# A gated cellular automaton beside the coupled map of its own image, its result in DRAM for the gate, and the gate's VectorE operations behind the first half of a map step

## The chip, the cores and the metric

The kernel runs on one core of a Trainium2 chip. The metric is device time in microseconds of one execution, lower is better. The page and the trace come from one profiled execution.

## The reference

Four layers run over 32 images of 8 channels, 256 x 256, each as `x = x + conv_i(group_norm(x))`. The change lies in layer 0; layers 1 to 3 (a quantized 3x3 convolution, a 3x3 convolution, a 5x5 box filter) stay as they are. Layer 0, cut to what matters:

```python
def _L0_conv_ref(x, K_local, Wp, bp, Wu, bu, Wg1, bg1, Wg2, bg2):
    drive = x[:, :C_OUT]
    grid = drive
    for _ in range(STEPS):                      # 15 steps
        mapped = R * grid * (1.0 - grid)
        local = _conv(mapped, K_local, groups=C_OUT)
        physics = (1.0 - EPS) * mapped + EPS * local
        grid = (1.0 - BETA) * physics + BETA * drive
    cml_out = jnp.clip(grid, 0.0001, 1.0 - 0.0001)
    h = jax.nn.relu(_conv(x, Wp, bp))           # 128 hidden channels
    nca_out = jax.nn.sigmoid(_conv(h, Wu, bu))
    gin = jnp.concatenate([x, cml_out, nca_out], axis=1)
    g = jax.nn.sigmoid(_conv(jax.nn.relu(_conv(gin, Wg1, bg1)), Wg2, bg2))
    return g * cml_out + (1.0 - g) * nca_out
```

So an image has three parts: the *map* (15 dependent steps giving `cml_out`), the *automaton* (`nca_out`, which depends on the normalized image alone), and the *gate*, which needs both.

## The kernel before, in words

**The map** is `lattice(b, ahead)`. The image is normalized (L346 into `flat`, L360 in place), turned by 32 TensorE transposes (L355), and six of the eight channels are stepped on TensorE, in two halves of three channels. For a half, TensorE multiplies the state by `patch_sb` (L391), then the ring of neighbours from other patches by `ring_sb` (L393); VectorE adds the drive (`psc`, L402); ScalarE squares into `state` (L419); `spread(half)` then issues four DMAs on SP's queue (L259), which fill `rings` for the same half of the next step. The other two channels are stepped by VectorE with nine taps (L338, over `strip` and `acc`): three taps in a step's first half, six in its second, where two closing operations (L412, L413) follow. After step 15 the result is turned back (L428, L431) and stored to `cr_d` (`store`, four DMAs on POOL's queue, and eight of SP's for the two VectorE channels).

**The automaton** is in `gated()`, in chunks `n` of 1/8 image; a chunk has four *batches*. `load` brings a batch's `im` tile in six DMAs on POOL's queue out of `xn_d`, where the normalized image lies in DRAM. Each batch has four matmuls `ph` (L633, 8 profile records), a relu to `hh` (L638), and a group of matmuls `pn` (L610). `close` turns the chunk's `pn` by a sigmoid into `nh` (L588), an SBUF tile with room for four chunks; the gate's neighbour rows are copied from it by `beside_blocks` (L480).

**The gate** is the generator `gate`: it loads its quarter of an image (`xq`, `cq`, the neighbours `above` and `below`, `xc`), issues 18 matmul records of `pg` (L531, L543), four with the neighbours (L539), a relu (L545), `pq` (L548), a sigmoid `gt` (L550), and seven VectorE operations (L561 to L568) that mix, add to `xc` and take statistics; the result goes to `x1_d` (L569). After an image's eighth gate its statistics are finished.

**What sets the order.** All of layer 0 is under a hand-written schedule: an instruction stands on its engine's queue where the Python code issues it. `lattice` yields gaps in microseconds of TensorE work to be filled; for each, the main loop draws pieces of `gated()`:

```python
for gap in lattice(b, ahead):
    if b > 0:
        left += gap
        while left > 0 and place[0] < b * NCH:
            left -= next(rest)
```

So during the map of image b the automaton and the gates of image b - 1 are issued, wherever they fall; the map of image 0 has nothing beside it, and the automaton and gates of image 31 come after the last map. `errands(b)` is drawn once a half: it writes image b to `xn_d` (four DMAs, L273) and `nr_d`, loads image b + 1 and takes its statistics. In its ScalarE part `lattice` issues, channel by channel, a square into `state` (L374) and the lift of the drive (L375), and then the `spread` of a half.

Of the kernel before, what the change touches and what calls it, by code (L numbers as in the profile page):

```python
# [18 lines left out]
C = 8  # L19
# [47 lines left out]
def kernel(  # L67
# [100 lines left out]
    with ExitStack() as es:  # L168
        wt = es.enter_context(tc.tile_pool(name="wt0", bufs=1))
        imp = es.enter_context(tc.tile_pool(name="im", bufs=4))  # L170
# [49 lines left out]
        nh = wt.tile([P, 8, WP], F32, name="nh")  # L220
# [7 lines left out]
        for t in (*xbs, nh, zero, strip):  # L228
            nc.gpsimd.memset(t, 0.0)
# [7 lines left out]
        nr_d = [dram.tile([P, HB, WP], F32, name=f"nr_d{i}") for i in range(3)]  # L237

        cr_d = [dram.tile([P, HB, WP], F32, name=f"cr_d{i}") for i in range(3)]
        for t in xn_d:  # L240
            nc.sync.dma_start(
                window(t, 0, [[HP * WP, C], [(HP - 1) * WP, 2], [1, WP]]),
                nh[0:C, 0:2, :],
            )
# [21 lines left out]
        def errands(b):  # L266
# [3 lines left out]
            if b >= 0:  # L270
                xb = xbs[b % 2]
                for r in four:
                    nc.gpsimd.dma_start(  # L273
                        window(
                            xn_d[b % 3], (1 + r.start) * WP,
                            [[HP * WP, C], [RB * WP, HB], [1, 4 * WP]],
                        ),
                        xb[:, r, :].rearrange("p r w -> p (r w)"),
                    )
                    yield  # L280
# [47 lines left out]
        def lattice(b, ahead):  # L328
# [8 lines left out]
            def tap(dy, dx):  # L337
# [8 lines left out]
            nc.vector.tensor_scalar(  # L346
                flat.rearrange("p (x r w) -> p r x w", x=TX, r=RB),
                xi.rearrange("p r (x w) -> p r x w", w=PW),
                st[:, 0:1], st[:, 1:2], ALU.subtract, ALU.mult,
            )  # L350
            yield 5
            for t4 in range(TX // 4):
# [6 lines left out]
                if t4 == 0:  # L359
                    nc.vector.tensor_scalar(  # L360
                        xi, xi, st[:, 0:1], st[:, 1:2], ALU.subtract, ALU.mult
                    )
                if t4 == 4 and b > 0:
                    store(b - 1)
                if t4 == 1:
# [4 lines left out]
                    edges()  # L370
                yield 1
            dr = flat.rearrange("p (x c y) -> p c x y", x=TX, c=C)
            for c in range(CP):
                nc.scalar.activation(inner(c), dr[:, c], AF.Square, bias=minus)  # L374
                nc.scalar.activation(  # L375
                    dr[:, c], dr[:, c], AF.Identity, bias=lift[:, c : c + 1], scale=BETA_
                )
                if c == 0:
                    nc.scalar.mul(d2, d2, BETA_)
                if c % HALF == HALF - 1:  # L380
                    spread(c // HALF)
                yield 1.5
            yield 4
            for step in range(STEPS):
                for half in range(2):
# [31 lines left out]
                    if step < STEPS - 1:  # L417
# [3 lines left out]
                        if half == 1:  # L421
                            edges()
                    next(ahead, None)
                    yield BLOCK - 1.7
            for t4 in range(TX // 4):
# [10 lines left out]
                )  # L436
                yield 1
# [25 lines left out]
        def beside_blocks(tiles, src, q, k0, n, slots):  # L463

            row = src.shape[1] * WP
            for i, (p, k) in enumerate(((P - C, k0 - 1), (0, k0 + 1))):
                to = tiles[i][q : q + 24, k0 % 4 : k0 % 4 + n, :].rearrange("p k w -> p (k w)")
                runs = []  # L470
                for j in range(n):
                    at = slots[k + j] if 0 <= k + j < HB else None
                    if runs and at is not None and runs[-1][2] is not None and at == runs[-1][2] + runs[-1][1]:
                        runs[-1][1] += 1
                    else:
                        runs.append([j, 1, at])
                for j, m, at in runs:
                    long = m * WP - 2
                    source, row_, start = (zero, WP, 0) if at is None else (src, row, p * row + at * WP)
                    nc.gpsimd.dma_start(  # L480
                        to[:, j * WP : j * WP + long],
                        window(source, start, [[row_, C], [1, 3], [1, long]]),
                    )

        place = [0]

        def gated():
# [5 lines left out]
            SLOTS = [k % 8 for k in range(HB)]  # L493
# [17 lines left out]
            def gate(n, quarter):  # L511
                b, r2 = divmod(n, NCH)
                k0 = 2 * r2
                if r2 % 2 == 0:
                    for name, t in (("xq", nr_d), ("cq", cr_d)):
# [3 lines left out]
                    for q, t in ((0, nr_d), (24, cr_d)):  # L519
                        beside_blocks(halos[n // 2], t[b % 3], q, k0, 4, range(HB))  # L520
                xc = hp.tile([P, 2, W], F32, name="xc", bufs=2)
                nc.gpsimd.dma_start(xc, xr_d[b % 3][:, k0 : k0 + 2, :])
                yield 0
                yield 0
                mine = slice(2 * (r2 % 2), 2 * (r2 % 2) + 2)
                xq, cq = (quarter[i][:, mine, :] for i in ("xq", "cq"))
                pg = ps_n.tile([P, 512], F32, name="pg", tag="pn")
                o = pg.rearrange("p (k w) -> p k w", w=W)
                for s, src in enumerate((xq, cq, nh[:, k0 % 8 : k0 % 8 + 2, :])):
# [14 lines left out]
                g1 = hp.tile([P, 512], F32, name="g1", tag="gt", bufs=2)  # L544
# [4 lines left out]
                gt = hp.tile([P, 2, W], F32, name="gt", tag="gt", bufs=2)  # L549
# [8 lines left out]
                ci = cq[:, :, 1 : 1 + W]  # L558
                ni = nh[:, k0 % 8 : k0 % 8 + 2, 1 : 1 + W]

                nc.vector.tensor_tensor(ci, ci, ni, ALU.subtract)  # L561
                nc.vector.tensor_tensor(gt, gt, ci, ALU.mult)
# [96 lines left out]
        with tc.manual_schedule():  # L659
# [15 lines left out]
            for _ in rest:  # L675
                pass
# [366 lines left out]
```

## Time and profile before

| what | value |
|---|---|
| median of 3 runs (lowest, highest) | 16326.91 us (16326.64, 16338.44) |
| profiled execution, its own time | 16318.33 us |
| its span, mean granted clock | 16316.6 us, 0.961 |
| PE, DVE, ACT, POOL busy | 95%, 72%, 35%, 34% |
| DMA | 2276.12 MB, 139 GB/s mean |
| first start of L346 for image 0, image 1 | 33.8, 381.7 us |
| last transposes back (L428); last gate sigmoid (L550) start | 13342.7; 13589.0 us |

The time of interest runs from the start to about 13,595 us, where layer 0 ends; the remaining 2,720 us are layers 1 to 3. The page cuts the span into 40 slices of some 408 us, close to one image of layer 0. PEclk in it is the granted share of TensorE's clock.

### The profile page before, as it was taken

The numbers are of one execution on the slowest core, as the hardware profiler recorded it, in microseconds if no ns is written. First come the engines' busy times: TensorE is split into PE (matmuls) and PEld (weight loads), VectorE is DVE, ScalarE is ACT, GpSimd is POOL, SyncE is SP. The second block draws the span as 40 slices with busy tenths as digits, with TensorE's granted clock in tenths as the row PEclk, the third lists the DMA queues.
The fourth block names the chain that finished last, engine by engine and source line by source line (L and its number), as shares of the span: only waits on it lengthen the run. The fifth ranks groups of instructions, "written<-read, shape, count | busy, mean of one in ns | idle before, by whom it ended". The sixth has DMA issues, their size and how long they took to land.

```text
span 16316.6 us, 141125 instructions
## 1 busy us (share of the span) xinstructions
PE 15452.2 (95%) x42888; PEld 6215.7 (38%) x42888; DVE 11705.9 (72%) x14652; ACT 5726.7 (35%) x8862; POOL 5598.2 (34%) x9491
## 2 busy tenths in 40 slices
PE   6999999999999999999999999999999997999999
PEld 2333333333333333333333333333333332333333
DVE  7777777777777777777777777777777764555554
ACT  2433444443434434443434444343444442111110
POOL 1333333333333333333333333333333342111111
PEclk7999999999999999999999999999999998999999
DMA  4766666666666666666666666666666664555554
GB/s 104 148 146 144 150 147 144 147 150 146 149 144 148 150 147 147 144 147 145 147 142 149 148 144 147 141 148 146 147 149 147 146 134 98 119 119 119 119 118 105
DMA packets 1057742, 2276.12 MB, mean 139 GB/s; under 512 B 419740, under 2 KB 623508, under 8 KB 1050724
## 3 DMA queue, kind: packets, MB, share of 16 engines
q0 software_dynamic: 704512, 1492.80, 40.6%
q1 hardware_dynamic: 352484, 774.29, 23.4%
q8 instruction: 356, 5.83, 0.2%
q14 instruction: 390, 3.19, 0.1%
HBM read 1078.04 MB, written 471.38 MB: 95 GB/s over the span
## 4 chain that ended last, share of the span: by engine, by line
PE 74%; DVE 13%; DMA 7%; ACT 3%; issue 2%; SPq 1%; POOL 0%; DVEq 0%; ACTq 0%; POOLq 0%
PE ph L633 17%; PE psc L391 14%; PE psc L393 13%; PE pg L531 9%; DVE acc L338 7%; PE psv L725 5%; PE pn L610 5%; PE psv L811 4%; DMA qb<-qh 3%; DMA rings<-state 2%; PE psv L729 2%; PE pq L548 1%; PE pg L543 1%; PE pg L539 1%; DVE psc L402 1%
## 5 line engine op out<-in xcount | busy, mean ns | idle before, releaser
L338 DVE SCALAR_TENSOR_TENSOR acc<-strip,taps_sb,acc 128x1024 f32<-128x1024 f32 x3840 | 4930.4, 1284 | 124.8 <-DMA strip<-strip 4.7
L505 POOL DMA_DIRECT2D im<-xn_d x6144 | 3458.3, 566 | 3250.0 <-PE ph L633 1434.7
L633 PE MATMUL ph<-im,wp_sb 72*128 72x512 f32 x8192 | 4091.7, 615 | 308.8 <-ACT hh L638 251.3
L638 ACT ACTIVATE hh<-ph,bp_sb 128x512 f32<-128x512 f32 x4096 | 2755.8, 690 | 4441.9 <-PE ph L633 4385.7
L402 DVE SCALAR_TENSOR_TENSOR psc<-psc,flat 128x512 f32<-128x512 f32 x2880 | 1921.4, 696 | 2813.0 <-PE psc L393 2797.2
L391 PE MATMUL psc<-state,patch_sb 128*128 128x512 f32 x5760 | 2812.0, 626 | 74.1 <-ACT state L419 63.3
L393 PE MATMUL psc<-rings,ring_sb 80*128 80x512 f32 x5760 | 2713.5, 607 | 129.8 <-DMA rings<-state 129.8
L633 PEld LDWEIGHTS ph<-im,wp_sb 72*128 72x128 f32 x8192 | 1489.5, 193 | 2425.4 <-issue 1587.8
L419 ACT ACTIVATE state<-psc,minus 128x512 f32<-128x512 f32 x2688 | 1690.2, 690 | 1818.8 <-DVE psc L402 1713.1
L391 PEld LDWEIGHTS psc<-state,patch_sb 128*128 128x128 f32 x5760 | 1114.5, 199 | 1696.2 <-issue 1375.7
L393 PEld LDWEIGHTS psc<-rings,ring_sb 80*128 80x128 f32 x5760 | 1114.7, 194 | 1576.8 <-issue 1545.7
L569 POOL DMA_DIRECT2D x_d<-xc x256 | 146.9, 574 | 3493.1 <-DVE xc L564 3416.6
L811 PE MATMUL psv<-xr,w_sb 128*128 128x512 f32 x2560 | 1162.9, 600 | 1.3 <-DVE xr L792 1.3
L610 PE MATMUL pn<-hh,wu_sb 128*32 128x512 f32 x8192 | 1133.9, 609 | 3.3 <-ACT hh L638 3.3
L776 POOL DMA_DIRECT2D x_d<-x x512 | 321.0, 643 | 1941.0 <-DVE x L770 1696.3
L725 PE MATMUL psv<-xh,w_sb 128*128 128x512 f32 x1536 | 753.0, 629 | 9.6 <-issue 9.6
L531 PE MATMUL pg<-xq,wg_sb 128*128 128x512 f32 x1536 | 749.3, 626 | 0.0
L754 ACT ACTIVATE x<-psv,b_sb,sc 128x512 f32<-128x512 f32 x256 | 199.3, 779 | 1466.2 <-PE psv L729 1465.8
L531 PE MATMUL pg<-cq,wg_sb 128*128 128x512 f32 x1536 | 713.7, 601 | 0.0
L811 PEld LDWEIGHTS psv<-xr,w_sb 128*128 128x128 f32 x2560 | 466.1, 189 | 610.8 <-issue 606.0
L338 DVE SCALAR_TENSOR_TENSOR acc<-strip,taps_sb,d 128x1024 f32<-128x1024 f32 x480 | 613.2, 1277 | 0.0
L831 DVE TENSOR_TENSOR y<-psv,y 128x512 f32<-128x512 f32 x256 | 177.1, 692 | 593.7 <-PE psv L811 593.7
(163 smaller groups left out, 12188.9 us busy)
## 6 DMA issues: line engine op xcount, KB each, us to landing
im<-xn_d POOLq DMA_DIRECT2D x6144, 96.6 KB, 6.6
rings<-state SPq DMA_DIRECT2D x1920, 159.5 KB
rings<-state SPq DMA_DIRECT2D x1920, 106.3 KB
strip<-strip SPq DMA_DIRECT2D x960, 126.0 KB
xn_d<-xb POOLq DMA_DIRECT2D x128, 516.0 KB, 7.7
nr_d<-xb POOLq DMA_DIRECT2D x128, 516.0 KB, 7.2
xq<-nr_d POOLq DMA_DIRECT2D x128, 516.0 KB, 5.1
cq<-cr_d POOLq DMA_DIRECT2D x128, 516.0 KB, 7.9
```

The lines of the kernel that those rows point to most:

```text
L338: nc.vector.scalar_tensor_tensor(acc, strip[:, dy : dy + RQ, dx : dx + W], taps_sb[:, 3 * dy + dx : 3 * dy + dx + 1], d2 if dy == 1 and dx ...
L391: nc.tensor.matmul(pss[-1], patch_sb[:, c, :], inner(c), start=True, stop=False)
L393: nc.tensor.matmul(pss[c % HALF], ring_sb[:, c, :], rings[half][:, c % HALF, 0 : TX * SY].rearrange("p (x y) -> p x y", y=SY)[:, :, 0:TY], ...
L402: nc.vector.scalar_tensor_tensor(ps, ps, FLOOR, dr[:, c], ALU.max, ALU.add)
L419: nc.scalar.activation(inner(c), pss[c % HALF], AF.Square, bias=minus)
L505: nc.gpsimd.dma_start(im[24 * dy : 24 * dy + 24, k, 0:run], window(xn_d[b % 3], at, [[HP * WP, C], [1, 3], [1, run]]),)
L531: nc.tensor.matmul(o, wg1_sb[:, s, dx, :], src[:, :, dx : dx + W], start=s == dx == 0, stop=False,)
L610: nc.tensor.matmul(pn[32 * q : 32 * q + 32, :], wu_sb[:, i, :], hh, start=i == 0, stop=i == 3,)
L633: nc.tensor.matmul(ph.rearrange("p (k w) -> p k w", w=W), wp_sb, im[:, :, j * WP : j * WP + W], start=True, stop=True,)
L638: nc.scalar.activation(hh, ph, AF.Relu, bias=bp_sb)
L725: nc.tensor.matmul(o, w[:, dx, :], src[:, 2 * i : 2 * i + 2, dx : dx + W], start=dx == 0, stop=False,)
L811: nc.tensor.matmul(pss[k].rearrange("p (c w) -> p c w", w=W), w3_sb[:, dx, :], xr[:, k, mine, dx : dx + W], start=dx == 0, stop=stop,)
```

## The change

- The automaton of image b is issued in the gaps of image b's own map. `place[0]` now counts batches, and `place[1]` is the batch up to which pieces may be drawn: to 32 b - 1 until the fifth group of transposes, from there to 32 (b + 1) - 3 (for the last image - 1). `nh` becomes two tiles, one a chunk; `keep_result` stores each to a new DRAM tensor `nh_d`, and the gate loads `nq` and its neighbours from there. A gate starts 31 batches after its chunk instead of 5, so gates of image b run beside the map of image b + 1; two more empty turns lie between its loads and its matmuls.
- The four writes to `xn_d` leave `errands` and stand in one block right after the normalization.
- The image is normalized in place first, and a `tensor_copy` then fills `flat`.
- All squares of a half are issued together and followed by its `spread`; the lifts come after.
- `im` has 3 buffers instead of 4, and `load` runs 2 batches ahead instead of 4.
- A gate's seven VectorE operations go into a list `spare`. `work(4)` issues up to four of them behind a step's first half (the three taps), `work(1)` one at a time among the transposes; `follow()` issues what comes after (the store to `x1_d`, the image's statistics) behind second halves.

```diff
-        imp = es.enter_context(tc.tile_pool(name="im", bufs=4))
+        imp = es.enter_context(tc.tile_pool(name="im", bufs=3))
-        nh = wt.tile([P, 8, WP], F32, name="nh")
+        nhs = [wt.tile([P, 2, WP], F32, name=f"nh{i}") for i in range(2)]
+        nh_d = [dram.tile([P, HB, WP], F32, name=f"nh_d{i}") for i in range(3)]
...
-            if b >= 0:
-                xb = xbs[b % 2]
-                for r in four:
-                    nc.gpsimd.dma_start(window(xn_d[b % 3], ...), xb[:, r, :]...)
-                    yield
...
-            nc.vector.tensor_scalar(
+            nc.vector.tensor_scalar(xi, xi, st[:, 0:1], st[:, 1:2], ALU.subtract, ALU.mult)
+            nc.vector.tensor_copy(
                 flat.rearrange("p (x r w) -> p r x w", x=TX, r=RB),
                 xi.rearrange("p r (x w) -> p r x w", w=PW),
-                st[:, 0:1], st[:, 1:2], ALU.subtract, ALU.mult,
             )
+            for r in range(0, RB, 4):
+                nc.gpsimd.dma_start(window(xn_d[b % 3], ...), xb[:, r : r + 4, :]...)
             yield 5
...
-                if t4 == 4 and b > 0:
-                    store(b - 1)
+                if t4 == 4:
+                    if b > 0:
+                        store(b - 1)
+                    place[1] = BATCHES * (b + 1) - (3 if b + 1 < B else 1)
...
+                if t4 > 1:
+                    work(1)
                 yield 1
+            follow()
+            for half in range(2):
+                for c in range(HALF * half, HALF * half + HALF):
+                    nc.scalar.activation(inner(c), dr[:, c], AF.Square, bias=minus)
+                spread(half)
+                yield 1.5
+            nc.scalar.mul(d2, d2, BETA_)
             for c in range(CP):
-                nc.scalar.activation(inner(c), dr[:, c], AF.Square, bias=minus)
                 nc.scalar.activation(dr[:, c], dr[:, c], AF.Identity, ...)
-                if c % HALF == HALF - 1:
-                    spread(c // HALF)
-                yield 1.5
+                yield 0.8
...
+                    if half == 0:
+                        work(4)
+                    else:
+                        follow()
                     next(ahead, None)
                     yield BLOCK - 1.7
...
+        def work(k):
+            for _ in range(min(k, len(spare))):
+                spare.pop(0)[1]()
+
+        def follow():
+            for n, parts in list(after.items()):
+                if next(parts, True):
+                    del after[n]
...
+                while spare and spare[0][0] <= n - 3:
+                    work(1)
                 if r2 % 2 == 0:
-                    for name, t in (("xq", nr_d), ("cq", cr_d)):
+                    for name, t in (("xq", nr_d), ("cq", cr_d), ("nq", nh_d)):
...
-                nc.vector.tensor_tensor(ci, ci, ni, ALU.subtract)
...
-                nc.vector.tensor_reduce(ext[:, 1, r2 : r2 + 1], flat, AX.X, ALU.min)
-                nc.gpsimd.dma_start(x1_d[b][:, bass.ts(r2, 512)], flat)
+                spare.extend((n, f) for f in (
+                    lambda: nc.vector.tensor_tensor(ci, ci, ni, ALU.subtract),
...
+                    last,
+                ))
...
+            def keep_result():
+                n = done.pop()
+                b, r2 = divmod(n, NCH)
+                nc.gpsimd.dma_start(nh_d[b % 3][:, 2 * r2 : 2 * r2 + 2, :], nhs[n % 2])
...
-                due.setdefault(batch + 5, []).append(gate(n, quarter))
+                due.setdefault(batch + BATCHES - 1, []).append(gate(n, quarter))
...
-                for gap in lattice(b, ahead):
-                    if b > 0:
-                        left += gap
-                        while left > 0 and place[0] < b * NCH:
-                            left -= next(rest)
-                        left = min(left, 0.0)
+                place[1] = BATCHES * b - 1
+                for k, gap in enumerate(lattice(b, ahead)):
+                    if b == k == 0:
+                        next(rest)
+                    left += gap
+                    while left > 0 and place[0] < place[1]:
+                        left -= next(rest)
+                    left = min(left, 0.0)
```

## The prediction, before the changed kernel ran

> **What bounds the kernel now.** I read the page from the top: engine sums, slices, then windows by stage, waits, and the timeline where a wait stands.
>
> ```profile
> PE 15452.2 (95%) x42888; PEld 6215.7 (38%) x42888; DVE 11705.9 (72%) x14652; ACT 5726.7 (35%) x8862; POOL 5598.2 (34%) x9491
> ...
> PE   6999999999999999999999999999999997999999
> ...
> PEclk7999999999999999999999999999999998999999
> ```
>
> TensorE bounds it, but slices 1 and 33 show it short of work: the map of image 0 alone at the start, the automaton and gates of image 31 alone at the end of layer 0. Windows over those two, one image in the middle (3718:4138), its calm part, and four places of loss in it:
>
> ```profile
> core 0: us, PE busy (x) PEld busy (x) DVE busy (x) ACT busy (x) POOL busy (x), PEclk, DMA share, GB/s
> 36.00:388.00 352.00, 226.61 (x452) 95.48 (x453) 283.87 (x304) 73.48 (x112) 28.66 (x45) 0.75 0.44 92
> 3718.00:4138.00 420.00, 403.38 (x1140) 161.10 (x1140) 318.04 (x373) 167.91 (x263) 160.64 (x277) 0.97 0.69 146
> 13343.00:13590.00 247.00, 245.11 (x758) 88.25 (x756) 50.06 (x88) 111.40 (x162) 138.39 (x247) 1.00 0.51 123
> 3744.00:3764.00 20.00, 13.98 (x25) 5.67 (x25) 2.43 (x4) 5.80 (x10) 7.45 (x13) 0.77 0.92 149
> 3784.00:3804.00 20.00, 16.85 (x37) 6.50 (x36) 14.10 (x18) 4.31 (x7) 8.96 (x16) 0.83 0.66 153
> 4052.00:4072.00 20.00, 15.50 (x38) 5.59 (x37) 13.58 (x18) 6.42 (x11) 11.20 (x20) 0.83 0.75 154
> 4123.00:4138.00 15.00, 12.32 (x54) 6.60 (x48) 9.91 (x14) 2.24 (x4) 5.95 (x11) 0.89 0.51 122
> 3860.00:3960.00 100.00, 99.89 (x277) 40.12 (x274) 86.89 (x109) 40.49 (x64) 40.71 (x70) 1.00 0.79 178
> ```
>
> The calm part has PE at 99.89 of 100 us and clock 1.00: no gain there. A place costs its idle time plus (1 - PEclk) x its window, less where they overlap: at most 10.6 us at 3744 (a DMA wait), 6.6 at 3784, 7.9 at 4052, 4.3 at 4123. The waits of PE give the owners over the run:
>
> ```profile
> PE ph L633 <- ACT hh L638: 251.3, 122, 4.9
> PE psc L393 <- DMA rings<-state: 129.8, 37, 18.9
> ...
> PE ph L633 <- DVE xb L431: 57.1, 30, 1.9
> ```
>
> The first is the one at 3784 and 4052: 8.1 us an image over 31. ACT is no true owner, as the timeline at 3784 shows:
>
> ```profile
> 3784.61 2.31 PE L393 MATMUL psc<-rings,ring_sb 80*128 80x512 f32 x5
> ...
> 3787.63 0.68 DVE L561 TENSOR_TENSOR cq<-cq,nh 128x512 f32<-128x512 f32 x1
> ...
> 3791.72 0.68 DVE L568 TENSOR_REDUCE ext<-xc 128x1 f32<-128x512 f32 x1
> 3792.31 1.89 DVE L402 SCALAR_TENSOR_TENSOR psc<-psc,flat 128x512 f32<-128x512 f32 x3
> 3793.04 1.89 ACT L419 ACTIVATE state<-psc,minus 128x512 f32<-128x512 f32 x3 [10.55 <-DVE psc L402]
> ...
> 3795.55 2.07 PE L633 MATMUL ph<-im,wp_sb 72*128 72x512 f32 x2 [3.15 <-ACT hh L638]
> ```
>
> Seven gate operations (L561 to L568, 4.8 us) stand behind six taps and the two closing ones of a second half. The psc tile, whose matmuls began at 3784.2, gets VectorE at 3792.3; the squares wait for it, the relu `hh` stands behind them in ACT's order, and PE runs out of psum tiles.
>
> **The skill.** "TensorE: Matmul & The Clock Gate", Part 1: about 3.4 us of an idle PE halve its clock until a busy window passes. The trace agrees: 3.15 us idle leave PEclk at 0.83 over 20 us. The same page (Architectural detail) calls ACT and DVE strict FIFO, which the queueing above shows. "VectorE: DVE Perf Modes", What auto-detection actually checks: a single source with both sides in SBUF can use both ports, in fp32 too. The trace agrees for tensor_scalar (4096 elements in 2399 ns, L346, while 512 of a tensor_tensor take 692); the new tensor_copy it does not show.
>
> **The change, part by part.** Orders are those of the built programs; PE work is records times 0.43 us, their spacing at full clock. A half is 12 records, 5.2 us; a batch 8 ph records and the pn group, 4.3; a gate 18 records, 4 of halo that go two at a time, 2 of pq, 9.5.
>
> 1. *Ends.* Image 0's map gets 29 batches of its own automaton, no gates. Before: 352 us from first transpose to first transpose of image 1, with the first ring matmul at 67.5, then 10.0 us a half ((367.4 - 67.5)/30). After: batch 0 stands behind 20 of 32 transposes and waits for the xn_d write and its im load: 4 issues and a landing of 7.7, then 6 issues of 0.57 and 3 to 6.6, less the copy beside them: 12 us taken (8 to 18); earlier squares give back 4. 18 halves then carry 5.9 us of batches each: 11.3 instead of 10.0, +23; 12 stay at 10.0. With 2.4 for the new copy: **+36** (20 to 55). The tail has 32 batches and 10 gates before (232 us of work in 247) and 7.75 batches and 11 gates after: 33 + 104 = 137, with 20 of waits (10 to 40): **-90** (-100 to -70). All PE work remains; what goes is the idle of image 0.
> 2. *Middle images.* (13343 - 381.7)/31 = 418.1 us each. PE work per image falls by 0.9, since the batches are spread over 32 maps.
> 3. *Gate operations.* Four behind the three taps of a first half, three in the next step's. First half: 3 x 0.70 + 3 x 1.28 + 4 x 0.69 = 8.7 us; second: 2.1 + 7.7 + 0.69 + 1.23 = 11.7, with two bn_stats 12.5; a half lasts 12.3 (L393 at 3757.4 and, 29 halves on, at 4114.2). So DVE is never over 1 us late, and the places at 3784 and 4052 go: 6 us each, 12 an image (8 to 14.5). If that cover failed, the wait would return in the second half.
> 4. *Image start.* Squares ahead of the lifts: in the traced image first square to first ring DMA took 5.6 us (three lifts and the d2 scaling between), which becomes some 2.2, while the ring matmuls stay 27 us after the first transpose. Against that, the four xn_d writes (2.06 MB) now come in a burst ahead of the four cr_d stores, where DMA share was already 0.92 at 149 GB/s; spread over four halves they cost nothing. Ring wait: -3.5 us (-8 to +7).
> 5. *Copy before the transposes.* 2.4 us by L346 (4.5 if it ran at single rate), with 3.4 to 7.7 us of PE fill ahead: +0.8. At the image end up to three gate operations stand between copies of the end transposes, +0.7 on the place at 4123.
> 6. *nh through DRAM.* 256 stores and 128 nq loads come, 576 small halo DMAs become 256: POOL's DMAs 9472 to 9536, 36 us of issue on an engine 34% busy; 135 MB more of 2276. POOL no longer waits for nh (below L480, 830.2 us over the run). On no path: 0; its cover is that rows are stored 31 batches before use.
> 7. *im: 3 buffers, loads 2 batches ahead.* Inside the steps 2 batches are about 25 us, against 6 issues and 6.6 to landing: 0. At the image start they are some 17 us, and the loads stand behind the xn_d, cr_d and gate DMAs on POOL: 0 taken, up to 10.
>
> Sum of a middle image: -0.9 - 12 - 3.5 + 0.8 + 0.7 = -14.9, times 31: -462. With the ends: -462 + 36 - 90 = -516; I take **-505**, since image 1 still waits for its first im. The profiled execution's own time is 16318.3 (span 16316.6), 8.6 under the median of 16326.9: 15,813 there, **15,820** as a median.
>
> **Rivals.**
> A. *Only the ends pay.* The burst at the image start costs as much as the two places give: +36 - 90 and some, about -60: 16,265. For it: DMA share 0.92 there. Against: half of the loss has nothing to do with DMA.
> B. *Slower: POOL's order at the image start.* im loads with 3 buffers, behind four writes that wait for DVE's normalise, four stores and up to 14 gate DMAs, come late once and the rings a second time. 2.06 MB at 149 GB/s are 14 us; both waits that long and two half-clock stretches of 6.8 us (3.4 lost each) make 35 us less some 4 of overlap: 31 - 14.9 + 36 - 90 over the run gives 31 x 16 - 54 = +445, 16,770. It decides from 16.6 us a middle image. For it: im loads took 10 to 13 us there already. Against: PE holds 14 to 17 us of work in hand.
> C. *The ring wait goes wholly,* with its half clock: another -4 an image: 15,700.
> D. *It doesn't do what it says:* gate operations behind second halves. In the built order they stand behind first halves in the images I went through. Then as A.
>
> **How the numbers follow.** Main case 0.58, C 0.17, A and D 0.12, B 0.13. The main case's bounds (two places 8 to 14.5, ring -8 to +7, ends) run from 15,630 to 16,100; taking in A the range is 15,620 to 16,270, with B left out. Faster by over 0.2% (33 us, about what a measurement of this kernel can tell from no change) 0.85, within 0.02, slower 0.13.
>
> **What would show it.** Right: image period near 403 us; PE's wait for ACT hh far under 251; slices 1 and 33 full or nearly; no gate operation between L412's and L401's of the changed kernel; tail of gates near 157 us. Wrong: ph waiting for DMA im, psc for rings longer than 130 in all, a new PEclk dip per image, period at 418 or above.

## The result, and the profile after

The changed kernel takes 16,376.6 us (median of 10 executions, 16,354.95 to 16,393.31) beside 16,326.8 us for the kernel before (10 executions): ratio 1.003, 95% interval 1.002 to 1.004. It is slower by 50 us, where 15,820 was forecast and 16,270 was the top of the range. The profiled execution took 16,354.95 us (span 16,353.2, mean clock 0.957).

The page of the changed kernel, the rows shown before:

```profile
PE 15413.2 (94%) x42888; PEld 6192.6 (38%) x42888; DVE 11697.8 (72%) x14652; ACT 5691.7 (35%) x8854; POOL 5637.8 (34%) x9556
...
PE   7999999999999999999999999999999997999999
...
PEclk9999999999999999999999999999999998999999
```

The first slice now has its clock (9 for 7) and more work (7 for 6); all other slices look as before. The dip in slice 34 stays: that slice covers 13,461 to 13,869 us, most of it in layer 1. Windows over image 0, image 13 and the tail, and then two short ones at the start of image 13 (columns as in the windows before):

```profile
core 0: us, PE busy (x) PEld busy (x) DVE busy (x) ACT busy (x) POOL busy (x), PEclk, DMA share, GB/s
37.80:438.80 401.00, 334.88 (x914) 134.46 (x914) 281.36 (x302) 149.94 (x237) 125.14 (x216) 0.89 0.60 126
5489.00:5910.00 421.00, 395.46 (x1092) 156.34 (x1094) 308.64 (x362) 163.38 (x257) 158.18 (x274) 0.94 0.68 154
13483.00:13629.00 146.00, 143.64 (x401) 54.23 (x399) 53.95 (x94) 41.88 (x60) 55.78 (x100) 1.00 0.48 135
...
5489.00:5509.00 20.00, 16.35 (x72) 7.83 (x72) 2.54 (x3) 16.25 (x27) 7.25 (x13) 0.99 0.75 173
5509.00:5529.00 20.00, 13.04 (x23) 3.64 (x24) 0.00 (x0) 4.75 (x8) 10.34 (x18) 0.50 0.81 205
```

Both ends moved about as forecast. A middle image did not: 421 us at a clock of 0.94, and in the last two lines the DMA engines move 173 and 205 GB/s at its start, where 149 was seen before (3744:3764), while PE falls to half clock. PE's waits over the run (line waited at, who ended it, us in all, times, longest):

```profile
PE ph L665 <- DMA im<-xn_d: 329.9, 63, 16.9
...
PE ph L665 <- DVE u L112: 43.4, 6, 8.0
PE ph L665 <- DVE stat L105: 42.0, 7, 6.7
...
PE ph L665 <- ACT hh L670: 14.7, 31, 3.0
...
PE psc L392 <- DMA rings<-state: 6.1, 7, 1.9
```

The wait for `hh` went from 251.3 to 14.7 us and that for the rings from 129.8 to 6.1: what the change was to take away is gone. Two new ones took over, for `im` (none among the rows of before) and for the statistics' pieces (`stat`, `u`). The timeline at the start of image 13, POOL's DMAs and the matmul that waited:

```profile
5486.95 4.06 POOL L342 DMA_DIRECT2D xn_d<-xb  x4 [12.48 <-DVE xb L336]
...
5491.00 0.60 POOL L599 DMA_DIRECT2D x_d<-xc  x1
...
5503.94 0.58 POOL L543 DMA_DIRECT2D xc<-xr_d  x1 [12.34 <-DMA x_d<-xc]
...
5504.53 3.34 POOL L521 DMA_DIRECT2D im<-xn_d  x6
5507.86 0.73 POOL L459 DMA_DIRECT2D cr_d<-xb  x1
...
5515.96 3.75 PE L665 MATMUL ph<-im,wp_sb 72*128 72x512 f32 x4 [10.48 <-DMA im<-xn_d]
```

POOL stands 12.5 us until VectorE has normalized, issues the four `xn_d` writes, then stands another 12.3 us because the `xc` load needs a buffer whose store, begun at 5491.00, travels with those writes. For some 30 us no `im` load is issued; PE waits 10.5 us for one.

### The profile page after: what moved, and what is told of

Read it like the earlier page. It is cut to its first block, busy times and chain, and to the rows that moved or that the text cites. A ratio compares the mean times of both kernels' runs of the same rounds, so it can differ in the third digit from the quotient of the medians.

```text
span 16353.2 us, 141124 instructions
## 1 busy us (share of the span) xinstructions
PE 15413.2 (94%) x42888; PEld 6192.6 (38%) x42888; DVE 11697.8 (72%) x14652; ACT 5691.7 (35%) x8854; POOL 5637.8 (34%) x9556
## 4 chain that ended last, share of the span: by engine, by line
PE 76%; DMA 12%; DVE 7%; issue 2%; POOL 2%; ACT 1%; SPq 0%; DVEq 0%; ACTq 0%; POOLq 0%
PE ph L665 19%; PE psc L390 14%; PE psc L392 14%; PE pg L552 9%; PE pn L642 5%; PE psv L767 5%; PE psv L853 4%; DMA qb<-qh 3%; DVE acc L328 3%; DMA im<-xn_d 3%; DMA xn_d<-xb 2%; PE psv L771 2%; PE pg L564 1%; PE pg L560 1%; PE pq L569 1%
## 5 line engine op out<-in xcount | busy, mean ns | idle before, releaser
L665 PE MATMUL ph<-im,wp_sb 72*128 72x512 f32 x8192 | 4212.2, 629 | 507.7 <-DMA im<-xn_d 329.9
L390 PE MATMUL psc<-state,patch_sb 128*128 128x512 f32 x5760 | 2719.9, 608 | 27.5 <-ACT state L418 19.8
L392 PE MATMUL psc<-rings,ring_sb 80*128 80x512 f32 x5760 | 2634.1, 592 | 6.1 <-DMA rings<-state 6.1
L543 POOL DMA_DIRECT2D xc<-xr_d x256 | 145.3, 568 | 1927.2 <-DVE ext L584 1244.6
## 6 DMA issues: line engine op xcount, KB each, us to landing
xn_d<-xb POOLq DMA_DIRECT2D x128, 516.0 KB, 12.1
```

Source lines behind the costliest of these rows:

```text
L390: nc.tensor.matmul(pss[-1], patch_sb[:, c, :], inner(c), start=True, stop=False)
L392: nc.tensor.matmul(pss[c % HALF], ring_sb[:, c, :], rings[half][:, c % HALF, 0 : TX * SY].rearrange("p (x y) -> p x y", y=SY)[:, :, 0:TY], ...
L665: nc.tensor.matmul(ph.rearrange("p (k w) -> p k w", w=W), wp_sb, im[:, :, j * WP : j * WP + W], start=True, stop=True,)
```

## The experiments

Each kernel below ran together with the kernel before on one chip, and the chips were not the same throughout; the medians of the kernel before lie between 16,297 and 16,323 us. So kernels that did not run together are compared by their ratios to it. "Period" is the mean distance between first transposes from image 1 to image 31 in the trace: 418.2 us before, 421.3 after; the "tail" runs from the last transposes back to the last gate sigmoid. "Half clock" is the sum of the stretches that the clock record shows at 0.5: 1,283 us before, 1,405 after. In the trace of before a `ph` matmul record takes 590 ns at the least and 1,222 at the most, so half of a stretch's length is taken for its price below; this is an estimate, and an upper one, since PE also waits in such stretches.

### Within the changed kernel: the writes, the xc load, the statistics, the place of the gate operations

```diff
 e1: -                nc.gpsimd.dma_start(window(xn_d[b % 3], ...
     +                nc.sync.dma_start(window(xn_d[b % 3], ...
 e2:                  for _ in range(4):
                          yield 0
     +                xc = hp.tile(...); nc.gpsimd.dma_start(xc, ...)   # was ahead of the loop
 e3:                  if half == 0:
     +                    follow()
                          work(4)
     -                else:
     -                    follow()
 e4:  behind spare.extend(...):
     +                work(7)
     +                follow()
```

> The changed kernel with its four xn_d writes an image issued from SP's queue instead of POOL's; nothing else moves. Theory 1 (POOL's one queue: the im loads stand behind writes that wait for DVE's normalization, 9.4 us of POOL idle an image in the profile after): ph's wait for DMA im falls from 330 us to about 120, and the time by 200 to 300 us, to some 16,120. Theory 2 (bandwidth: 2 MB in one burst, whoever issues them): the wait stays near 330 and the time within 30 us of the changed kernel's 16,377.

> The changed kernel with the gate's xc tile taken and loaded four batches later, just ahead of the gate's matmuls, so that its wait on POOL for the buffer (for DVE's last gate operation three gates earlier, and for the x1_d store) is over by then. If that wait is what holds the im loads (POOL idles 1244.6 us before xc for L584 alone): ph's wait for DMA im falls by a third or more and the time by 80 to 200 us. If it only fills time that POOL has to spare: within 30 us of 16,377.

> The changed kernel with follow() called in the first half, ahead of work(4), and not in the second. Theory 3 (the statistics' psum tile, filled by PE L104 or L111 in the second half, is freed by DVE only behind six taps and two closing operations, so ph runs out of psum tiles): PE's waits for DVE stat L105, u L112 and t L108, 121 us together, fall under 40, and the time falls by 100 to 180 us. Rival (the same operations are late wherever they stand): unchanged within 30 us.

> The changed kernel with the seven gate operations issued at once where the gate's sigmoid has been issued, as in the kernel before, and the store to x1_d behind them; all else as changed. If step 3 of the prediction holds (two places of some 6 us an image removed by the placement): PE's wait for ACT hh comes back to about 250 us and the time rises by 250 to 400 us, to some 16,700. If the placement bought nothing here: within 40 us of 16,377.

| kernel | median us | ratio to before (interval) | period us | PE's wait for im, us |
|---|---|---|---|---|
| e1, xn_d writes on SP | 16,239 | 0.9956 (0.9942 to 0.9971) | 416.8 | 240.4 |
| e2, xc load later | 16,359 | 1.0028 (1.0015 to 1.0041) | 421.5 | 290.7 |
| e3, statistics in first halves | 16,279 | 0.9978 (0.9971 to 0.9985) | 418.9 | 339.8 |
| e4, gate operations in place | 16,533 | 1.0137 (1.0122 to 1.0152) | 426.5 | 329.9 |

e1 shows the four writes in POOL's queue to cost 4.4 us an image, e3 the statistics in second halves 2.4. e2 takes away nearly all of POOL's standing at `xc` (1,927.2 us over the run after, 216.9 in e2), and the time moves by no more than the intervals. Its trace shows why, here at the start of image 13, whose first transpose starts at 5532.43:

```profile
5530.26 4.06 POOL L342 DMA_DIRECT2D xn_d<-xb  x4 [12.53 <-DVE xb L336]
...
5535.48 1.16 POOL L521 DMA_DIRECT2D im<-xn_d  x2
...
5550.49 1.26 POOL L521 DMA_DIRECT2D im<-xn_d  x2 [7.91 <-DMA xn_d<-xb]
...
5557.88 3.75 PE L665 MATMUL ph<-im,wp_sb 72*128 72x512 f32 x4 [9.09 <-DMA im<-xn_d]
```

The first loads of the batch go out 12 us earlier than in the changed kernel, but POOL now stands for the `xn_d` writes to land, since it never has more than eight DMAs in flight (see the last section). The batch's last load lands 25.3 us after the first transpose instead of 26.7. So it is not the `xc` load that holds the batch up, but the writes ahead of it. In e1 they stand in SP's queue (first transpose at 5467.68):

```profile
5465.23 5.70 SPq L342 DMA_DIRECT2D xn_d<-xb  x4
...
5465.32 5.26 POOL L521 DMA_DIRECT2D im<-xn_d  x6
...
5487.13 0.56 POOL L521 DMA_DIRECT2D im<-xn_d  x1 [2.82 <-DMA cr_d<-xb]
...
5499.61 2.04 PE L665 MATMUL ph<-im,wp_sb 72*128 72x512 f32 x2 [8.10 <-DMA im<-xn_d]
```

The batch has landed after 12.8 us and PE does not wait for it; but the loads of the next batch stand behind the `cr_d` stores, and PE waits 8.1 us there. So the wait for `im` fell to 240 us over the run and not to the 120 that was expected. The writes also change from the profile's software queue of DMAs to its hardware queue; what that does by itself was not tried.

e4 is the surprise: to put the gate operations back costs about 175 us by the ratios (1.0137 beside 1.0030) and not 250 to 400. In this kernel the deferral is worth 5 us an image.

### The two repairs together, the cr_d stores spread; two parts of the change on the kernel before

e5 is e1 and e3. e6 adds this, and a start of the gates eight batches later:

```diff
 in lattice:   -  store(b - 1)              # at the fifth transpose group
 in errands:   +  yield from store(b - 1)   # one of the four DMAs a half
               -  due.setdefault(batch + BATCHES - 1, ...
               +  due.setdefault(batch + BATCHES + 7, ...
```

e7 is the kernel before with `im` at 3 buffers and its loads one batch later (counted from the batch being issued: three ahead before, two in the changed kernel). e8 is e7 with the gate operations in `spare`, `work(4)` and `follow()` in first halves and `work(1)` among the transposes. It also gives `xc` three buffers instead of two and `g1` and `gt` buffers of their own, as the changed kernel does.

> The changed kernel with both edits that helped: the four xn_d writes on SP's queue, and the statistics' pieces in the first half ahead of the four gate operations. Theory (two separate losses: im loads held back at an image's start by POOL's order, and PE held mid-image by the statistics' psum tiles that VectorE frees late): the gains add, -137 - 97 against the changed kernel, some 16,140, ratio 0.988; PE's waits for stat, u and t of the statistics under 30 us together, ph for DMA im about 240. Rival (one slack fills the other, since the automaton's own pace then bounds the image): 16,210 or more, and the wait of psc for the rings or for hh grows.

> The two edits of e5_both, and the four cr_d stores of the image before are no longer issued at the fifth transpose group but one a half in the first four halves (as the kernel before spread its xn_d writes); the gates start eight batches later so that they still follow the stores, which puts two more gates (19 us) behind the last image. Theory (what is left of the im wait, 240 us, is the transfer of two bursts of 2.06 MB in the same 25 us): ph for DMA im falls under 120, the period by 3 to 5 us, some 60 to 100 us less than e5_both after the 19: about 16,060. Rival (own image's xn_d burst alone keeps the loads late, or the loads stand behind their own buffers): im stays over 200, time at e5_both's plus 19 or so.

> The kernel before with nothing changed but im: 3 buffers instead of 4, its loads 2 batches ahead instead of 3. The prediction took 0 for this step (up to 10 us an image). If that holds: 16,320 within 0.2%, ph for DMA im under 20 us over the run. If the depth by itself costs at the image's start: ph for DMA im 100 us or more, 16,400 or above. Then part of the loss of the changed kernel is the smaller buffer and not the burst.

> The kernel before with the seven gate operations put off to the first halves (four in each, as in the changed kernel), the statistics' pieces in the first half too, xc with 3 buffers, gt and g1 apart, and im with 3 buffers so that it fits; map, xn_d writes, squares and nh as before. The prediction's step 3 (two places of 6 us an image go): against e7_before_im3 -12 x 31 = -370, and PE's wait of ph for ACT hh from 251 to under 60; about 15,950 if e7 is 16,320. Rival (what was waited for there is passed on: the automaton's rings or VectorE's later taps take the time): less than -150 against e7.

| kernel | median us | ratio to before (interval) | period us | half clock us |
|---|---|---|---|---|
| e5, e1 and e3 | 16,130 | 0.9896 (0.9879 to 0.9913) | 412.8 | 1,136 |
| e6, and cr_d stores spread | 15,921 | 0.9764 (0.9738 to 0.9790) | 406.7 | 948 |
| e7, before with im 3 | 16,514 | 1.0130 (1.0106 to 1.0154) | 425.8 | 1,555 |
| e8, before with the gate part | 15,833 | 0.9713 (0.9689 to 0.9737) | 403.2 | 828 |

The gains of e1 and e3 add (1.0030 - 0.0074 - 0.0052 = 0.9904; e5 has 0.9896). The spread stores give another 6.0 us an image: two bursts at once, of 2.06 MB (`xn_d`) and 1.55 MB (`cr_d`, four times 387 KB and not the 2.06 of the expectation), cost more at an image's start than POOL's order. e6 also starts the gates later, but the gain lies where the bursts were: 20 to 40 us after the first transpose, half clock falls from 324 us in e5 to 89 in e6, and PE's idle time from 161 to 59 (images 1 to 30), while half clock rises by 46 us in the rest of these images. (Without the `xn_d` block a like step gives 1.5: e11 beside e9, below.) PE's waits of e6, e7 and e8, in this order:

```profile
PE ph L668 <- DMA im<-xn_d: 125.2, 32, 16.0
```

```profile
PE ph L633 <- ACT hh L638: 249.8, 120, 4.9
PE psc L393 <- DMA rings<-state: 124.7, 34, 18.4
...
PE ph L633 <- DMA im<-xn_d: 91.9, 28, 5.7
```

```profile
PE psc L396 <- DMA rings<-state: 114.7, 63, 18.6
...
PE ph L663 <- ACT hh L668: 20.5, 62, 2.6
```

e8 has the period that was forecast for the whole change, by chance: it leaves out the squares, and gains where the forecast saw nothing to gain. It gains nearly twice what was expected beside e7, and e7 loses 217 us where 0 was taken: with gate operations in place, a buffer less makes PE wait 91.9 us for `im`. With gates deferred and the same 3 buffers no such wait is among PE's.

### The squares alone, the x1 store, the statistics on the kernel before

```diff
 e9  (on e8):  the loops of squares and lifts as in the changed kernel
 e10 (on e7), e15 (on before):
     -                nc.gpsimd.dma_start(x1_d[b][:, bass.ts(r2, 512)], flat)
     +                nc.sync.dma_start(x1_d[b][:, bass.ts(r2, 512)], flat)
 e11 (on e9):  store(b - 1) out of the transposes into errands, two DMAs a half; due: batch + 7
 e12 (on e8):  follow() in second halves, as in the changed kernel
```

> e8_before_gate with one more part of the change: the squares and their ring transfers ahead of the lifts at an image's start, while the xn_d writes stay spread as in the kernel before. Step 4 of the prediction without its burst: the ring wait of 114.7 us (63 times) of e8 goes, with the half clock after it, -3.5 us an image, about 15,725 beside e8's 15,833. Rival (the ring transfers are late because the four cr_d stores fill the DMA engines, whenever they are issued): ring wait over 80 us, time within 30 us of e8's.

> e7_before_im3 with the store of each gate's result (x1) on SP's queue instead of POOL's. Theory: with 3 buffers the im loads came late because POOL stood at that store, waiting for VectorE's gate operations, with the im loads queued behind it; then the 217 us of e7 go, ph for DMA im from 92 to under 20 us, time 16,300 within 0.3%. Rival (3 buffers are too few for the loads' own flight, or the store held up the gate's xc load): time stays over 16,450. SP may in turn hold ring transfers behind the store: psc for rings up to 200 would show that.

> e9_gate_squares with the four cr_d stores two a half in the first two halves instead of together at the fifth transpose group, gates two batches later. If the burst of cr_d is what keeps the rings or PE at 20 to 40 us into an image, that place falls from 1.9 us idle and 7.1 us of half clock to under 0.5 and 2, -3 to -5 us an image: 15,600 to 15,700. If e9 has taken that wait already, equal to e9 within 30 us; if the stores collide with xn_d's writes in the halves after, slower than e9 and ph for DMA im appears.

> e8_before_gate with the statistics' pieces in the second halves, where the changed kernel has them; this is the changed kernel's treatment of the gate operations alone on the kernel before, with im at 3 buffers. If the pieces' place costs the same here as in the changed kernel (97 us there): 15,930, with PE waiting for stat, u and t of the statistics 100 us or so. If the changed kernel's loss needed the late image start: within 30 us of e8's 15,833.

> The kernel before with one line changed: the store of each gate's result (x1) on SP's queue. If POOL's standing at that store (3,416 us over the run in the trace of before) is what cost e7 its 217 us, and 4 buffers only hid a part of it, this gains about what e10 gained on before: 16,050 to 16,100. If 4 buffers hid it wholly, 16,300 within 0.3%, and e10's gain over the kernel before (209 us) came from elsewhere.

| kernel | median us | ratio to before (interval) | period us | tail us | half clock us |
|---|---|---|---|---|---|
| before | | 1 | 418.2 | 246.3 | 1,283 |
| e9, e8 and squares first | 15,759 | 0.9664 (0.9649 to 0.9678) | 399.2 | 279.9 | 716 |
| e11, and cr_d stores spread | 15,710 | 0.9631 (0.9617 to 0.9646) | 397.7 | 287.0 | 655 |
| e12, e8 with statistics in second halves | 15,828 | 0.9698 (0.9678 to 0.9717) | 402.4 | 247.7 | 821 |
| e10, e7 with the x1 store on SP | 16,091 | 0.9866 (0.9848 to 0.9884) | 411.5 | 246.3 | 1,006 |
| e15, before with the x1 store on SP | 16,104 | 0.9874 (0.9857 to 0.9890) | 411.3 | 246.3 | 965 |

e10 and e15 are equal within their intervals: once POOL does not stand at the store, the fourth `im` buffer makes no difference. So e7's loss was the store with the loads behind it and a buffer less to cover it, and not the depth by itself. The first line is POOL's of the kernel before; the second fence is PE's of e15:

```profile
POOL x_d L569 <- DVE xc L564: 3416.6, 242, 36.0
```

```profile
PE ph L633 <- ACT hh L638: 250.6, 122, 4.5
...
PE psc L393 <- DMA rings<-state: 59.4, 28, 18.8
```

In e15 the wait for `hh` is untouched. What fell is the ring wait (129.8 to 59.4) and the half clock (1,283 to 965 us, priced at half): 70 + 159 = 229 beside 206 measured. Most of it lies in one place: half clock that begins 20 to 40 us after an image's first transpose fell from 307 to 65 us (images 1 to 30). At image 9 of the kernel before, POOL stands 3.2 us at the store, then issues six `im` loads and the four `cr_d` stores, the last of them 9.7 us after the first transpose; in e15 the last goes out after 5.8 us, and PE's wait of 5.6 us for the rings there is gone. So what counts is a few microseconds at the image's start, and not the 36 us that the store can stand elsewhere. POOL's standing as such does not go away: in e15 it stands at the next `xc` loads (1,291.4 us for `psc` alone). That the late stores are what made the rings late is read from these times; no run moved them alone on the kernel before. The store, too, changes from the software to the hardware queue.

e9 prices step 4's squares without its burst: -4.0 us an image, of which 33/31 = 1.1 is work that now falls into the tail. e12 is e8 within the intervals: the statistics' place costs nothing on the kernel before. There VectorE answers PE as late (image 13: matmul 163.6 us after the first transpose, copy at 173.4), but PE hardly waits for it. One difference stands in the traces. A gate first issues whatever the third gate before it still has in `spare` (`while spare and ...: work(1)`). In the changed kernel this puts 294 of the 1,792 gate operations, three at a time, behind the closing operations of 98 second halves; in e8 and e12 it puts none there. Of the 121 us for which PE waited for the statistics' pieces in the changed kernel, 75 fall within 8 us of these halves. That the gates' place causes them was not tried.

### What is left of the changed kernel's loss

e13 breaks up an even gate's 14 loads in e6 (`yield 0` behind `cq` and behind the first halos, two empty turns for odd gates), e14 does the like in e11; e16, e17 and e18 are e6, e11 and e13 with the x1 store on SP.

> e6_both_store with an even gate's 14 loads on POOL issued in three parts, a batch apart (odd gates two batches later too), so that im loads stand between them. Theory (the block of gate loads, of which eight at most are in flight, keeps the im loads that stand behind it late): ph for DMA im from 125 to under 50 us, period from 406.3 to 402 or less, 15,780 to 15,830. Rival (the automaton's own image needs its loads before POOL can give them, whatever the order): im over 100, time within 40 us of e6's 15,921.

> e11_gate_squares_store with an even gate's loads (xq and cq, then the halos of each) issued a batch apart. e11 shows next to no wait for im, so equal to it within 30 us (15,710) is expected; if POOL's block also delays xn_d writes or x loads there, some 30 to 60 less. Beside e13 it tells what moving the map to its own image is worth once its queue costs are gone: the prediction had -54 for the ends.

> e6_both_store with the x1 store on SP's queue. POOL waited 322 us at it in e6, mostly beside other waits: 15,900 to 15,921 expected, a little less than e6 at most; ph for DMA im about 110. If POOL's store wait also held the im loads at the image start (10 us at 28 us into image 14), up to 70 us less.

> e11_gate_squares_store with the x1 store on SP's queue. POOL's waits show no standing at the store in e11, so equal to 15,710 within 30 us; the rings may lose a little to the store on their queue.

> e13_both_store_spread with the x1 store on SP's queue. If POOL's standing at the store is the cause of e13's loss, the 271 us go and the broken-up loads show what they are worth alone: 15,780 to 15,930, ph for DMA im under 110. If gates two batches later cost by themselves (VectorE's operations forced out in a lump), it stays above 16,050 with ph for ACT hh near 68.

| kernel | median us | ratio to before (interval) | period us |
|---|---|---|---|
| e13, e6 with loads in parts | 16,192 | 0.9929 (0.9914 to 0.9943) | 414.9 |
| e14, e11 with loads in parts | 15,780 | 0.9678 (0.9662 to 0.9694) | 399.0 |
| e16, e6 with the x1 store on SP | 15,950 | 0.9770 (0.9756 to 0.9785) | 406.7 |
| e17, e11 with the x1 store on SP | 15,685 | 0.9614 (0.9598 to 0.9630) | 396.1 |
| e18, e13 with the x1 store on SP | 16,254 | 0.9962 (0.9947 to 0.9977) | 416.8 |

The theory behind e13 fell: it is 271 us slower than e6. I took the store for the reason, since POOL's first wait in e13 is the first line below (322 us in e6); e18 shows that the store alone isn't it. With the store on SP the wait only changes its owner: POOL stands at the next reader of the same gate's result, the `cq` load (third line, e18), and SP stands 1,529.3 us at the store with the rings behind it (second line, PE's wait in e18).

```profile
POOL x_d L609 <- DVE xc L601: 2929.5, 214, 27.7
```

```profile
PE psc L393 <- DMA rings<-state: 174.2, 41, 10.9
```

```profile
POOL cq L541 <- DVE gt L599: 1820.6, 118, 25.7
```

e14 is slower than e11 too, by 70 us, and there POOL stands 1,418.6 us at the store. What both edits did to VectorE's order stands in the traces: in e13, 200 gates have their seven operations in one block, 14 in e6; in e14 94, in e11 none. With the loads in parts a gate's operations come into `spare` so late that the `while` line above soon forces them out together. So the edit took back most of the deferral, and the queues that need the operations stand. This was e18's second expectation (above 16,050, `hh` near 68; measured 16,254 and 80.4). Whether an even gate's block of loads, by itself, holds up `im` in e6 stays open, for e13 did not change that alone. So does the rest of the changed kernel's loss: e16 and e17 differ by 10.6 us an image with the store on SP in both. They differ in the own-image automaton with its `xn_d` writes in one block, the `nh` way through DRAM and the copy, and these were not taken apart further. The 98 second halves with gate operations behind them (e6 has as many) are not the reason: PE's waits near them sum to 18.7 us in e6. What the move gives is small: its ends save 51.5 us in the changed kernel.

e17 beats both kernels: 15,685 us, 3.9% under the kernel before by its ratio, and the changed kernel is slower than that. It keeps the change's treatment of the gate operations and of the squares, leaves the automaton one image behind, spreads the `cr_d` stores, and takes the x1 store off POOL. Its intervals overlap e11's, so the last of these is not shown to matter there; nor is it in e16 beside e6.

## Why the prediction was wrong, by its steps

1. *Ends*: right together. First transposes of image 0 to those of image 1 took 351.5 and now 401.1 us, +49.6 for +36 (range 20 to 55; the terms that are listed add up to 33 or 34); the tail 246.3 and now 145.2, -101 for -90 (range -100 to -70). Together -51.5 for -54, so the two errors cancel. The second dip of PE's row was misread: it is slice 34, and from its start to the last gate sigmoid PE was busy 127.1 of 129 us.
2. *Middle images*: this sum is where the forecast failed. Its period was 403.2; counted in its way it was (13,483.2 - 432.3)/31 = 421.0. 17.8 us times 31 are 552 of the 557 us missed.
3. *Gate operations*: the wait for `hh` goes as the step says (20.5 us over the run in e8), and alone on the kernel before the part gives -15.0 us an image for -12. What the step didn't see is that POOL stood behind the same operations: 6.9 of such a gain are to be had without moving any of them (e15). How the 15.0 divides between VectorE and POOL was not measured, so the nearness to 12 is in part luck. The row of POOL's 3,416.6 us was in the profile of before; I did not ask what stood behind it. The order was not wholly as stated either: 294 operations stand behind second halves (above), which is rival D in small; PE's wait for `hh` stays at 14.7 us all the same.
4. *Image start*: **the step that failed, together with step 7.** The ring wait fell as said (6.1), and squares first give -4.0 (e9; 1.1 of it is work that moves into the tail) for -3.5. But the burst's price was looked for at the rings alone, within -8 to +7; it fell on the `im` loads, which are in the same queue and travel with it, and for which step 7 took 0. The writes in POOL's queue cost 4.4 (e1), both bursts at once 6.0 (e6 beside e5): 10.4 of the 22 us an image that the changed kernel has over e9.
5. *Copy*: right. It took 2.29 us for 2.4 (4.5 at single rate), and PE's wait for `flat` was 17.2 us over the run. The +0.7 at the image's end does not show: PE's waits for `xb` sum to 71.8 us before and 72.1 after.
6. *nh through DRAM*: not shown. POOL no longer waits for `nh`, and what the 14 gate loads cost in its place is in the part left open.
7. *im*: "0 taken, up to 10" was this case's real term. PE waited 329.9 us for `im`, 10.6 an image, with half clock after it. On the kernel before, the depth by itself costs nothing where POOL does not stand at the store (e10, e15); what failed is the step's cover, that POOL would get to the loads in time. The step named what the loads stand behind and still priced it at nothing. Four buffers in the changed kernel were not tried.

A cost outside all steps was the place of the statistics: `follow()` in second halves, 2.4 (e3) to 4.1 us (e5 beside e1).

So the periods add along the kernels that were run: 399.2 with gates and squares alone (e9), +7.6 for the own-image automaton and what comes with it (e6; 9.0 beside e11, whose `cr_d` stores are spread as in e6), +6.0 for both bursts at once (e5), +4.1 for the statistics (e1), +4.4 for the writes on POOL: 421.3. The forecast for gates and squares was right to 4 us. Of the 22 us on top, 10.4 came from the writes and bursts at the image's start, 4.1 from the statistics, and 7.6 are not explained.

Rival B named the mechanism (POOL's order at the start, `im` late) and the sign. It doubled the wait by making the rings late a second time, which the trace refutes, and so came out at 16,770, too high, and was given 0.13. The signs of failure were the right ones: `ph` waits for DMA `im`, the clock dips anew at each image's start, and the period is above 418.

The Trainium skill, "DMA: Bandwidth & Descriptors", Issuing engines are not separate DMA queues, says that to issue on several engines saves only the sequencer's time, which is usually small. Here it was not: one store per gate on another queue took 206 us off the kernel before (e15), four writes an image took about 121 off the changed one (e1, by the ratios). What was saved is more than the time to issue: the `im` loads no longer stood behind those transfers; the bytes stayed the same. That all transfers share the DMA engines, which the same section says, fits e6.

## What to carry to other kernels

In these traces an engine issues its DMAs in order, and one that waits holds up all behind it: for each DMA that waits for another engine, ask what stands behind it, and give it another queue or a later place if that is on the path. If a write is moved from a spread place into one block, price what is issued behind the block and what travels with it, not only its reader. If a change has several parts, put the promising one alone on the kernel before: here that gave as much as was forecast for the whole, and the other parts took it back.

## What the runs showed of the hardware

In these traces POOL never had more than eight DMAs in flight: in the first 13,000 us of the kernel before 2,995 of 8,394 issues found seven still travelling and none found more. 1,200 of the idle stretches of over 0.3 us ahead of an issue ended within 0.45 us of the landing of the eighth-last DMA, 1,671 us in all (1,177 and 1,865 us after the change). So slow transfers cost a queue twice: the four `xn_d` writes landed after 12.1 us (median; 7.7 before) and took half of the eight places for as long. The eight come from the program: POOL's DMAs report their landing on eight semaphores in strict turn (1,184 DMAs each), and in each of those stretches the issue waits for the semaphore that it is to use itself, which the eighth-last DMA raises. Whether the chip would take more in flight, no run tells.

Half clock is a large part of each loss. From e7 to e17 it falls from 1,555 to 617 us: priced at half, 469 us of the 840 between their ratios.
